# An attention layer's gathers: end rows picked by turned one-hots on TensorE, a small table for the other ends, and mixing by group with an operand in PSUM

## The chip, the cores and the metric

The kernel runs on one core of one Trainium2 chip. The metric is device time in microseconds for one execution; three runs of the kernel before gave 4565.82, 4569.41 and 4575.6 us, median 4569.41. The profile is of one further execution.

## The reference

12500 nodes with 256 features, 200000 edges (src, dst) sorted by dst. Two residual blocks follow each other: a graph convolution network and an attention layer. Cut to what matters:

```python
# block 0: y = two graph convolutions (sum over edges and self loop, scaled by degree) between two dense layers
h = relu(layernorm(x))
x = x + gcn(h)                       # out[d] = sum over edges (s, d) of norm * (h @ W)[s], twice
# block 1: attention
h = relu(layernorm(x))
xt = (h @ weight).reshape(-1, 4, 64)             # 4 heads of 64
alpha_l = einsum('ehd,hd->eh', xt[src], attn_l)
alpha_r = einsum('ehd,hd->eh', xt[dst], attn_r)
alpha = softmax(leaky_relu(alpha_l + alpha_r, 0.01), axis=1)
tmp = einsum('nh,nhd->nd', alpha[:n], xt[dst[:n]])   # edge i of the first n = 12500 edges goes to node i
x = x + broadcast(tmp to the 4 heads)
```

So the attention uses the first 12500 edges only. Since the edges are sorted by dst, their dst ends are a few low node numbers, whereas their src ends lie anywhere.

## The kernel before, in words

Nodes are cut into NT = 98 tiles of P = 128, edges into NCH = 112 chunks of CE = 1792 = J x P edges, J = 14. The program is written in the order in which each engine executes it; the tile framework adds the semaphores, but doesn't reorder.

*Preparation* (lines 484 to 757) loads the edges, brings them to the layout "edge on partition" (src_t, dst_all; base_b is the first dst of each chunk, repeated on all partitions), counts degrees, and norms x into table1 in HBM. Lines 753 to 755 make the index tiles dst_i and al_i of the attention.

*Two convolutions* (`convolve`, line 776) run over all 1563 edge tiles. For each, POOL issues an indirect DMA that gathers 128 rows of the table (`fgot`, L871, 64 buffers ahead), and PE multiplies them by a one-hot matrix of the chunk (`fhot`, made by DVE at L815) into an accumulator (L876). After a chunk `close` copies the sums out, turns them (L828) and adds them into a sliding buffer (L838). When the buffer's first 128 nodes are complete, `shift` opens the next window (L850, L851) and puts the steps of `finish` on a list `due`; each step has a due time counted in edge tiles, and `run` emits what is due after each tile. After the last tile `run()` emits the rest in the order of due times: this is the drain. If two windows are complete at once, the second is shifted J = 14 tiles later (line 860).

`finish2` (line 921), for the second convolution, has the steps a to r: SP loads the self rows, a root row and x rows (L933, L935, L939), then come two dense layers (fpz L952, fpo L964), x2 is stored in `kept_x` (SP, L971), normed, turned and multiplied by the attention weights with attn_l and attn_r folded in (fpx, L997, 264 columns: 256 of xt, 4 left, 4 right), copied (L1002) and written by ACT's queue to table3 (L1003). The PSUM tiles fpt, fpz, fpo and fpx have one buffer each.

*Attention* (lines 1012 to 1059) runs over NG = 14 groups of G = 7 node tiles. For each tile POOL gathers the 264 columns of the dst row (L1021) and the 4 left columns of the src row, from table3 seen as rows of 4 (L1024). SP loads the group's x rows (L1028, three buffers). DVE adds the two terms, takes the leaky maximum and the softmax over the 4 heads (L1031 to L1041, the exponential on ACT), and then per tile multiplies, sums over the heads and adds to x (L1046, L1049, L1050). SP stores the group (L1056, the incomplete last tile by L1059). POOL and DVE run ahead by the buffers: 2 for the gathered rows, 3 for the left columns.

Of the kernel before, what the change touches and what calls it, by code (L numbers as in the profile page):

```python
# [17 lines left out]
P = 128  # L18
# [395 lines left out]
def fast_path(  # L414
# [41 lines left out]
    DA = D + 2 * H  # L456
    G = 7
# [12 lines left out]
    table3 = dram.tile([NT * P, DA], F32, name="ftable3")  # L470
# [15 lines left out]
    dst_i = const.tile([P, NT], I32, name="fdst_i")  # L486
    al_i = const.tile([P, NT], I32, name="fal_i")
# [10 lines left out]
    with tc.tile_pool(name="fprep", bufs=1) as prep, \  # L498
# [102 lines left out]
        base_b = prep.tile([P, NCH], F32, name="base_b")  # L601
# [65 lines left out]
        with tc.tile_pool(name="fln", bufs=2) as ln:  # L667
            for g in range(NG):
# [71 lines left out]
                for i in range(G):  # L740
# [12 lines left out]
        nc.vector.tensor_copy(dst_i, dst_all[:, :NCH, :].rearrange("p c j -> p (c j)")[:, :NT])  # L753
        nc.vector.tensor_scalar(al_i, src_t.rearrange("p c j -> p (c j)")[:, :NT],
                                float(DA // H), float(D // H), op0=ALU.mult, op1=ALU.add)
# [10 lines left out]
    with tc.tile_pool(name="fwork", bufs=2) as work:  # L766
        for i, a in enumerate((attn_l, attn_r)):
# [8 lines left out]
    def convolve(ep, table, stride, width, ahead, with_sum, psum, finish):  # L776
# [42 lines left out]
        def close(c, acc, t):  # L819
# [24 lines left out]
            def shift(now):  # L844
# [14 lines left out]
                if state["w"] < complete[c + 1]:  # L859
                    at(now + J, shift)  # L860
# [66 lines left out]
    def finish2(psum, w, buf, sbuf):  # L927
# [65 lines left out]

        def q():
            px = v["px"] = psum.tile([P, DA], F32, name="fpx", bufs=1)
            for k in range(KC):
                nc.tensor.matmul(px, v["ht"][:, k, :], wg[:, k, :],  # L997
                                 start=(k == 0), stop=(k == KC - 1))

        def r():  # L1000
            xa = work.tile([P, DA], F32, name="fxa")
            nc.scalar.activation(xa, v["px"], AF.Copy)  # L1002
            nc.scalar.dma_start(table3[w * P:(w + 1) * P, :], xa)  # L1003
# [3 lines left out]

    with tc.tile_pool(name="psum2", bufs=1, space=PSUM) as psum, \
            tc.tile_pool(name="edges2", bufs=1) as ep, \
            tc.tile_pool(name="fwork2", bufs=2) as work:  # L1010
        convolve(ep, table2, D, D, 64, False, psum, lambda w, b, s: finish2(psum, w, b, s))


    left = table3[:].rearrange("n (a h) -> (n a) h", h=H)
    with tc.tile_pool(name="fatt", bufs=2) as ap:
        for t0 in range(0, NT, G):
            g = min(G, NT - t0)
            xa = ap.tile([P, G, DA], F32, name="fxg", bufs=2)
            al = ap.tile([P, G, H], F32, name="fal", bufs=3)
            for j in range(g):  # L1020
                nc.gpsimd.indirect_dma_start(  # L1021
                    out=xa[:, j, :], out_offset=None, in_=table3[:],
                    in_offset=bass.IndirectOffsetOnAxis(ap=dst_i[:, t0 + j:t0 + j + 1], axis=0))
                nc.gpsimd.indirect_dma_start(  # L1024
                    out=al[:, j, :], out_offset=None, in_=left,
                    in_offset=bass.IndirectOffsetOnAxis(ap=al_i[:, t0 + j:t0 + j + 1], axis=0))
            xr = ap.tile([P, G, D], F32, name="fxr", bufs=3)
            nc.sync.dma_start(xr[:, :g, :], kept_x[t0 * P:(t0 + g) * P, :].rearrange(  # L1028
                "(c p) d -> p c d", p=P))
            s = ap.tile([P, G, H], F32, name="fs")  # L1030
            nc.vector.tensor_add(s[:, :g, :], al[:, :g, :], xa[:, :g, D + H:])  # L1031
            nc.vector.scalar_tensor_tensor(s[:, :g, :], s[:, :g, :], SLOPE, s[:, :g, :],
                                           op0=ALU.mult, op1=ALU.max)
            m = ap.tile([P, G], F32, name="fm")
            nc.vector.tensor_reduce(m[:, :g], s[:, :g, :], AX.X, ALU.max)
            nc.vector.tensor_sub(s[:, :g, :], s[:, :g, :],
                                 m[:, :g, None].to_broadcast([P, g, H]))
            nc.scalar.activation(s[:, :g, :], s[:, :g, :], AF.Exp)
            nc.vector.tensor_reduce(m[:, :g], s[:, :g, :], AX.X, ALU.add)
            nc.vector.reciprocal(m[:, :g], m[:, :g])  # L1040
            nc.vector.tensor_mul(s[:, :g, :], s[:, :g, :],  # L1041
                                 m[:, :g, None].to_broadcast([P, g, H]))
            res = ap.tile([P, G, D], F32, name="fres", bufs=2)
            for j in range(g):
                part = ap.tile([P, H, C], F32, name="fpart")
                nc.vector.tensor_mul(part, xa[:, j, :D].rearrange("p (h c) -> p h c", h=H),  # L1046
                                     s[:, j, :, None].to_broadcast([P, H, C]))
                mix = ap.tile([P, C], F32, name="fmix")
                nc.vector.tensor_reduce(mix, part.rearrange("p h c -> p c h"), AX.X, ALU.add)  # L1049
                nc.vector.tensor_add(res[:, j, :].rearrange("p (h c) -> p h c", h=H),  # L1050
                                     xr[:, j, :].rearrange("p (h c) -> p h c", h=H),
                                     mix[:, None, :].to_broadcast([P, H, C]))
            n0, n1 = t0 * P, min((t0 + g) * P, N)
# [4 lines left out]
            if r:  # L1058
                nc.sync.dma_start(out[n0 + k * P:n1, :], res[:r, k, :])  # L1059

# [40 lines left out]
```

## Time and profile before

| | us |
|---|---|
| median of the runs shown | 4569.41 |
| the profiled execution | 4561.96 |
| its span, first to last instruction | 4559.9 |
| PE busy | 3245.4 (71%) |
| POOL busy | 3182.4 (70%) |
| DVE busy | 1201.9 (26%) |
| ACT busy | 368.2 (8%) |
| first gather of the first convolution at | 288.86 |
| first gather of the second convolution at | 2270.95 |
| first gather of the attention at | 4282.26 |

An instruction group in the profile shows its line, engine, operation and tiles, its count, its busy time and the mean duration. The time of a gather on POOL is that of its issue, not of its transfer. Gathers: L871 3126 times at 954 ns, L1021 98 times at 987 ns, L1024 98 times at 996 ns. PE: L876 6252 times at 482 ns (each fp32 matmul is two instructions). DVE in the attention: L1046 419 ns, L1049 584 ns, L1050 426 ns, 98 each; L815 makes a chunk's one-hot in 2000 ns. The windows view gives the busy time of each engine in a stretch, the critical chain what each instruction on the path that ended last was released by, and the timeline every instruction in order.

### The profile page before, as it was taken

Reading aid. Unit: us, or ns where it says so; the run is one execution under the profiler, and the core shown is the slowest. Engines: PE = TensorE matmul, PEld = TensorE weight load, DVE = VectorE, ACT = ScalarE, POOL = GpSimd, SP = SyncE. Lnnn points to the kernel's source line nnn. Section 1 sums busy time; section 2 is a strip of 40 time slices with the busy share of each in tenths; the row PEclk is TensorE's granted clock in tenths of the full one; section 3 lists DMA queues with packets and bytes.
Section 4 is the critical chain, followed back from the end, with each engine's and each line's share of the span. In section 5 each row is a group of like instructions: output and inputs, shape, how many; then the busy total and the mean of one; then the engine's idle time right before and its main releaser. Section 6 shows DMA issues by size and latency. Waiting matters only on the chain.

```text
span 4559.9 us, 37494 instructions
## 1 busy us (share of the span) xinstructions
PE 3245.4 (71%) x12108; PEld 1986.7 (44%) x12108; DVE 1201.9 (26%) x2736; ACT 368.2 (8%) x956; POOL 3182.4 (70%) x3334
## 2 busy tenths in 40 slices
PE   4557777777777777777777888888878788778400
PEld 3533334434444443443345555555545555555200
DVE  4322222222222222222212222222222222222255
ACT  1210000000000000000001111111111111111100
POOL 0037777777777777777677777777777777777476
PEclk7558888888888888788879888888898998998655
DMA  2344444444444444444334444444444444444354
GB/s 76 115 119 119 119 119 120 120 120 119 119 119 122 118 120 118 120 121 118 108 116 132 130 130 131 130 134 129 130 133 129 132 129 134 128 132 129 92 152 144
DMA packets 302161, 561.52 MB, mean 123 GB/s; under 512 B 71717, under 2 KB 198564, under 8 KB 301956
## 3 DMA queue, kind: packets, MB, share of 16 engines
q0 software_dynamic: 157888, 426.59, 33.6%
q1 hardware_dynamic: 113918, 104.77, 7.5%
q10 hardware_dynamic: 30150, 27.68, 1.8%
q8 instruction: 98, 1.61, 0.1%
q14 instruction: 107, 0.88, 0.1%
HBM read 493.89 MB, written 64.78 MB: 123 GB/s over the span
## 4 chain that ended last, share of the span: by engine, by line
DMA 43%; PE 33%; issue 11%; POOL 7%; DVE 4%; ACT 1%; SPq 0%; POOLq 0%; ACTq 0%; DVEq 0%
DMA fgot<-ftable,fsrc_t 38%; PE facc L876 20%; POOL fgot L871 6%; PE fpz L952 2%; DMA fxt<-in_x_dram 2%; PE fpo L911 2%; PE fpz L954 2%; PE fpo L964 2%; PE fpx L997 1%; DMA fxr<-kept_x 1%; PE fpt L886 1%; PE fpo L912 1%; ACT h L741 1%; PE fpo L965 1%; DVE fmix L1049 1%
## 5 line engine op out<-in xcount | busy, mean ns | idle before, releaser
L871 POOL DMA_INDIRECT fgot<-ftable,fsrc_t x3126 | 2982.8, 954 | 1251.2 <-issue 717.2
L876 PE MATMUL facc<-fgot,fhot 128*128 128x257 f32 (+1 forms) x6252 | 2310.9, 482 | 874.7 <-DMA fgot<-ftable,fsrc_t 858.2
L876 PEld LDWEIGHTS facc<-fgot,fhot 128*128 128x128 f32 x6252 | 1167.3, 221 | 1853.3 <-DMA fgot<-ftable,fsrc_t 1675.4
L815 DVE TENSOR_TENSOR fhot<-iota_p,to_t 128x1792 f32<-128x1792 f32 x224 | 447.6, 2000 | 0.1
L969 DVE SCALAR_TENSOR_TENSOR fx<-fpo,fdinv,fxb 128x256 f32<-128x256 f32 x98 | 47.4, 484 | 1206.2 <-PE fpo L965 1206.2
L822 ACT ACTIVATE fsums<-facc 128x257 f32<-128x257 f32 (+1 forms) x224 | 86.2, 385 | 2914.1 <-PE facc L876 2914.1
L905 DVE TENSOR_TENSOR fin<-buf,fpt 128x256 f32<-128x256 f32 x98 | 41.3, 421 | 1010.8 <-PE fpt L901 1010.8
L838 DVE TENSOR_TENSOR buf<-buf,fturn 128x256 f32 x224 | 94.5, 422 | 641.2 <-PE fturn L830 530.9
L952 PE MATMUL fpz<-fin,fwb 128*128 128x128 f32 x784 | 157.9, 334 | 0.0
L1021 POOL DMA_INDIRECT fxg<-ftable,fdst_i x98 | 96.8, 987 | 72.0 <-PEq L1071 42.4
L911 PE MATMUL fpo<-wf,fin 128*128 128x256 f32 x392 | 139.4, 493 | 1.8 <-DVE fin L905 1.8
L952 PEld LDWEIGHTS fpz<-fin,fwb 128*128 128x128 f32 x784 | 130.9, 235 | 16.2 <-issue 5.7
L699 PE MATMUL count<-hot_a,hot_b 128*16 128x20 bf16 (+2 forms) x1591 | 62.2, 206 | 105.3 <-DVE hot_a L688 105.3
L997 PE MATMUL fpx<-fwg,ht 128*128 128x264 f32 x392 | 119.7, 434 | 0.5 <-ACT ht L992 0.5
L1024 POOL DMA_INDIRECT fal<-ftable,fal_i x98 | 97.6, 996 | 29.9 <-issue 29.2
L911 PEld LDWEIGHTS fpo<-wf,fin 128*128 128x128 f32 x392 | 102.4, 262 | 25.2 <-ACT fo L916 2.6
L964 PE MATMUL fpo<-fwo,fz 128*128 128x256 f32 x392 | 110.7, 409 | 0.0
L954 PE MATMUL fpz<-rm,fb2r 1*128 1x128 f32 x392 | 110.1, 366 | 0.0
L699 PEld LDWEIGHTS <-hot_b 128*16 128x16 bf16 x1591 | 61.7, 106 | 105.6 <-DVE hot_b L688 91.8
L997 PEld LDWEIGHTS fpx<-fwg,ht 128*128 128x128 f32 x392 | 85.4, 219 | 17.0 <-ACT ht L992 0.7
L828 PE MATMUL fturn<-fident,fsums 128*128 128x128 f32 x448 | 91.5, 288 | 0.0
L964 PEld LDWEIGHTS fpo<-fwo,fz 128*128 128x128 f32 x392 | 83.6, 213 | 15.6
(147 smaller groups left out, 1757.9 us busy)
## 6 DMA issues: line engine op xcount, KB each, us to landing
fgot<-ftable,fsrc_t POOLq DMA_INDIRECT x3126, 2.8
ftable<-fxa ACTq DMA_DIRECT2D x98, 132.0 KB
ftable<-h SPq DMA_DIRECT2D x14, 910.0 KB
self<-ftable SPq DMA_DIRECT2D x98, 130.0 KB
ftable<-fo ACTq DMA_DIRECT2D x98, 128.0 KB
self<-ftable SPq DMA_DIRECT2D x98, 128.0 KB
kept_x<-fx SPq DMA_DIRECT2D x98, 128.0 KB
fxr<-kept_x SPq DMA_DIRECT2D x14, 896.0 KB
```

The source lines that it names most:

```text
L699: nc.tensor.matmul(count[i][:, o:o + m], hot_b[:, :, t], hot_a[:, at:at + m, t], start=False, stop=False, skip_group_check=True)
L815: nc.vector.tensor_tensor(h[:, :n, :], iota_p[:, None, :].to_broadcast([P, n, P]), to_t[:, c, :n, None].to_broadcast([P, n, P]), ALU.is_equal)
L838: nc.vector.tensor_add(b, b, v["pt"][:, :KC, :])
L871: nc.gpsimd.indirect_dma_start(out=got, out_offset=None, in_=table[:], in_offset=bass.IndirectOffsetOnAxis(ap=src_t[:, c, j:j + 1], axis=0))
L876: nc.tensor.matmul(acc, hots[c][:, j, :], got[:, :width], start=(j == 0), stop=(j == nj[c] - 1))
L911: nc.tensor.matmul(po, v["f"][:, k, :], wf[:, k, :], start=(k == 0), stop=False)
L952: nc.tensor.matmul(pz[:, m, :], wb[:, k, m * P:(m + 1) * P], v["f"][:, k, :], start=(k == 0), stop=False)
L954: nc.tensor.matmul(pz[:, m, :], b2r[:, m * P:(m + 1) * P], v["rm"], start=False, stop=True)
L964: nc.tensor.matmul(po, v["z"][:, m, :], wo[:, m, :], start=(m == 0), stop=False)
L997: nc.tensor.matmul(px, v["ht"][:, k, :], wg[:, k, :], start=(k == 0), stop=(k == KC - 1))
L1021: nc.gpsimd.indirect_dma_start(out=xa[:, j, :], out_offset=None, in_=table3[:], in_offset=bass.IndirectOffsetOnAxis(ap=dst_i[:, t0 + j:t0 ...
L1024: nc.gpsimd.indirect_dma_start(out=al[:, j, :], out_offset=None, in_=left, in_offset=bass.IndirectOffsetOnAxis(ap=al_i[:, t0 + j:t0 + j + ...
```

## The change

Only what the attention reads is changed, and how it is made.

Two tables take the place of table3. `table_l` has the 4 left columns of all nodes. `table_r` has xt and the 4 right columns (260 columns) of the first XW = 9 windows only, which hold all dst ends of the AC = 7 chunks that the attention uses. Windows from the ninth on compute just 4 columns of fpx. For this the order of the folded columns is turned, right before left.

For each of the 7 chunks one indirect DMA gathers 128 rows of table_r, from the chunk's first dst onwards (`rows`). `turn_hots` loads the chunk's 1792 dst into every partition and compares them with base + partition: a one-hot with the row on the partition and the edge along the free side. `ends_of` then multiplies it, tile by tile, by the chunk's rows on PE and copies the result on ACT; it runs two groups ahead of `mix`. Three one-hots are made ahead of the second convolution, the other four when `ends_of` first needs them. POOL gathers only the left columns, directly by src.

`mix` does product, sum over heads and addition once per group of 7 tiles (1792 elements) instead of once per tile. The shares of the heads and the mixed sums lie in PSUM.

In both convolutions a second window that is complete at the end is shifted 3 tiles after the first instead of 14.

```diff
+    DR = D + H
-    table3 = dram.tile([NT * P, DA], F32, name="ftable3")
+    AC = -(-N // CE)
+    XW = (M * (AC - 1) + OFF + P - 1) // P + 1
+    table_r = dram.tile([XW * P, DR], F32, name="table_r")
+    table_l = dram.tile([NT * P, H], F32, name="table_l")
...
-        nc.vector.tensor_copy(dst_i, dst_all[:, :NCH, :].rearrange("p c j -> p (c j)")[:, :NT])
-        nc.vector.tensor_scalar(al_i, src_t.rearrange("p c j -> p (c j)")[:, :NT],
-                                float(DA // H), float(D // H), op0=ALU.mult, op1=ALU.add)
+        nc.vector.tensor_scalar(row_i, base_b[:, :AC], lane, float(XW * P - 1), op0=ALU.add,
+                                op1=ALU.min)
...
-                    at(now + J, shift)
+                    at(now + (J if c + 1 < NCH else 3), shift)
...
+        d0 = 0 if w < XW else DR
         def q():
             px = v["px"] = psum.tile([P, DA], F32, name="fpx", bufs=1)
             for k in range(KC):
-                nc.tensor.matmul(px, v["ht"][:, k, :], wg[:, k, :],
+                nc.tensor.matmul(px[:, d0:], v["ht"][:, k, :], wg[:, k, d0:],
                                  start=(k == 0), stop=(k == KC - 1))
         def r():
             xa = work.tile([P, DA], F32, name="fxa")
-            nc.scalar.activation(xa, v["px"], AF.Copy)
-            nc.scalar.dma_start(table3[w * P:(w + 1) * P, :], xa)
+            nc.scalar.activation(xa[:, d0:], v["px"][:, d0:], AF.Copy)
+            nc.scalar.dma_start(table_l[w * P:(w + 1) * P, :], xa[:, DR:])
+            if w < XW:
+                nc.scalar.dma_start(table_r[w * P:(w + 1) * P, :], xa[:, :DR])
...
+    def turn_hots(c):
+        to_all = ap.tile([P, CE], I32, name="to_all", bufs=2)
+        nc.sync.dma_start(to_all, dst[c * CE:(c + 1) * CE].partition_broadcast(P))
+        hot_t[c] = ap.tile([P, CE], F32, name="hot_t", bufs=3)
+        nc.vector.tensor_scalar(hot_t[c], to_all, base_b[:, c:c + 1], lane,
+                                op0=ALU.subtract, op1=ALU.is_equal)
...
+        for c in range(3):
+            turn_hots(c)
         convolve(ep, table2, D, D, 64, False, psum, lambda w, b, s: finish2(psum, w, b, s))
...
+        for c in range(AC):
+            rows.append(mp.tile([P, DR], F32, name="rows", bufs=AC))
+            nc.gpsimd.indirect_dma_start(
+                out=rows[c], out_offset=None, in_=table_r[:],
+                in_offset=bass.IndirectOffsetOnAxis(ap=row_i[:, c:c + 1], axis=0))
+        def ends_of(g):
+            xa = ends[g] = mp.tile([P, G, DR], F32, name="fxg", bufs=4)
+            for i in range(G):
+                c, j = divmod(g * G + i, J)
+                if j == 0 and c not in hot_t:
+                    turn_hots(c)
+                px = psum.tile([P, DR], F32, name="fends", bufs=4)
+                nc.tensor.matmul(px, hot_t[c][:, j * P:(j + 1) * P], rows[c], start=True,
+                                 stop=True)
+                nc.scalar.activation(xa[:, i, :], px, AF.Copy)
+        def mix(g):
+            xa, t0 = ends.pop(g), g * G
+            al = mp.tile([P, G, H], F32, name="fal", bufs=3)
+            for i in range(G):
+                c, j = divmod(t0 + i, J)
+                nc.gpsimd.indirect_dma_start(
+                    out=al[:, i, :], out_offset=None, in_=table_l[:],
+                    in_offset=bass.IndirectOffsetOnAxis(ap=src_t[:, c, j:j + 1], axis=0))
+            xr = mp.tile([P, G, D], F32, name="fxr", bufs=3)
+            nc.sync.dma_start(xr, kept_x[t0 * P:(t0 + G) * P, :].rearrange(
+                "(c p) d -> p c d", p=P))
...
+            share = psum.tile([P, G, H], F32, name="share")
+            nc.vector.tensor_mul(share, s, m[:, :, None].to_broadcast([P, G, H]))
+            part = mp.tile([P, G, H, C], F32, name="fpart")
+            nc.vector.tensor_mul(part, xa[:, :, :D].rearrange("p g (h c) -> p g h c", h=H),
+                                 share[:, :, :, None].to_broadcast([P, G, H, C]))
+            mixed = psum.tile([P, G, C], F32, name="fmix")
+            nc.vector.tensor_reduce(mixed, part.rearrange("p g h c -> p g c h"), AX.X, ALU.add)
+            res = mp.tile([P, G, D], F32, name="fres", bufs=2)
+            nc.vector.tensor_add(res.rearrange("p g (h c) -> p g h c", h=H),
+                                 xr.rearrange("p g (h c) -> p g h c", h=H),
+                                 mixed[:, :, None, :].to_broadcast([P, G, H, C]))
...
+        for g in range(NG + 2):
+            if g < NG:
+                ends_of(g)
+            if g >= 2:
+                mix(g - 2)
```

## The prediction

> **What bounds the kernel now.** I read the page's chain of waits first, then the busy time by windows, then the timeline around the last gather and the attention stage. The chain says which work the two convolutions hang on:
>
> ```profile
> DMA fgot<-ftable,fsrc_t 38%; PE facc L876 20%; POOL fgot L871 6%; PE fpz L952 2%; DMA fxt<-in_x_dram 2%; PE fpo L911 2%; PE fpz L954 2%; PE fpo L964 2%; PE fpx L997 1%; DMA fxr<-kept_x 1%; PE fpt L886 1%; PE fpo L912 1%; ACT h L741 1%; PE fpo L965 1%; DVE fmix L1049 1%
> ```
>
> The gathers and the matmuls waiting for them carry it. That it is the gathers' pace and not the matmuls' shows in the windows: POOL is busy equally in both convolutions, though PE has more to do in the second.
>
> ```profile
> 1000.00:1500.00 500.00, 374.28 (x1108) 205.17 (x1108) 110.01 (x236) 19.87 (x53) 378.78 (x399) 0.85 0.43 120
> 3000.00:3500.00 500.00, 409.21 (x1494) 268.67 (x1494) 125.17 (x255) 56.76 (x153) 379.05 (x398) 0.88 0.45 131
> 4300.00:4400.00 100.00, 0.00 (x0) 0.00 (x0) 57.21 (x151) 1.36 (x6) 76.44 (x78) 0.50 0.50 145
> ```
>
> After the window come PE, PEld, DVE, ACT and POOL with counts, clock, DMA share and GB/s. 398 gathers in 500 us are one per 1.25 us, so 1563 gathers make 1960 us per convolution. PE work removed there buys nothing.
>
> The third row is the attention stage: no PE, POOL at its full pace. It holds 14 groups of 7 node tiles, two gathers a tile. From the timeline it runs from 4282.26 (first gather) to 4559.9: 277.6 us, with 42 us of drain between the last edge gather at about 4240 and it. In the critical chain of one of its periods the reader should see that POOL is not alone:
>
> ```profile
> 4372.70 8.46 DMA fxr<-kept_x
> 4381.18 0.05 DVEq L1050
> ...
> 4389.76 0.44 DVE fres L1050
> 4390.22 0.38 SPq L1056
> 4390.59 0.05 issue
> 4390.64 8.47 DMA fxr<-kept_x
> ```
>
> SP works in order: the load of the next group's x rows (L1028) stands behind the store of this group's result (L1056), which waits for the last addition. The load takes 8.47 us, and only then can the 21 mixing operations (8.9 us) run on, since the first addition waits for it. 0.45 + 8.47 + 0.13 + 8.9 = 17.95 us; the 14 gathers need 14 x 1.25 = 17.5, more where they take 1.41. Two bounds nearly tie at 18 us per group, so a change has to lower both.
>
> **What the skill says.** SBUF, section "Who interferes with whom": a DVE instruction with two SBUF inputs contends with a GpSimd instruction that reads SBUF, one with a single SBUF input does not. The trace fits: an attention gather takes 0.94 us beside an idle DVE and 1.11 beside the mixing, whose multiplications and additions read two SBUF tiles. VectorE: DVE Perf Modes, "The perf-mode tier table": fp32 tensor_tensor and tensor_reduce run at one element a cycle, an SBUF tensor_scalar at two; here 1568 elements took 1.73 us in a tensor_tensor (L632) and 0.97 in a tensor_scalar (L607). DMA: Bandwidth & Descriptors, "Issuing engines are not separate DMA queues": all issuers share 16 engines. In the load's window they are 0.89 busy and 0.22 outside it:
>
> ```profile
> 4390.60:4399.10 8.50, 0.00 (x0) 0.00 (x0) 2.33 (x9) 0.23 (x1) 6.37 (x8) 0.50 0.89 264
> 4399.10:4408.20 9.10, 0.00 (x0) 0.00 (x0) 8.49 (x19) 0.00 (x0) 6.97 (x8) 0.50 0.22 61
> 4537.10:4544.20 7.10, 0.00 (x0) 0.00 (x0) 2.33 (x9) 0.23 (x1) 0.00 (x0) 0.50 0.85 260
> ```
>
> The third row is the last load, without gathers: load and store of 0.9 MB each keep 16 engines 0.85 x 7.1 = 6.0 us, 3.0 us each.
>
> **The change, part by part.**
>
> (1) Gathers of the attention: 196 become 7 (row ends) + 98 (L-table). The 7 need a table finished early and run in the drain, where POOL idles. The 98 keep the price of the present small gathers: 7 x 1.25 = 8.75 us a group.
>
> (2) Row ends on PE and ACT: 98 fp32 products of 260 columns and 98 copies. A pair of such matmuls took 0.43 us back to back and 0.9 at the half clock (L876); a copy of 264 took 0.39. A group is 3 to 6.3 us PE and 2.7 us ACT, below every other bound. The first three groups come ahead of the first mixing: 4 x 0.9 + 17 x 0.45 = 11 us from the end of PE's drain, which the first gathers cover.
>
> (3) Mixing by group on DVE: seven small operations and the exponential as now, 1.8 us (4301.06 to 4302.87). The product over 1792 elements with one PSUM operand: 2.0, the price of L815, which has the same size and a PSUM operand. The addition: 2.0 likewise. The reduction to 448 outputs in PSUM is not shown; L538 reduces 1792 to one in 2.0, and L1049 is 0.17 us over a plain 256-element operation for 64 outputs, or 2.6 ns an output, which makes 3.1. Bounds 2.2 (extra paid once) and 3.3; I take 3.1. Sum with gaps 9.05 us, instead of 1.8 + 7 x 1.41 = 11.7. What matters more: of this only the 2.0 us of addition now comes after the load.
>
> (4) An ordinary period is then 0.45 + load + 0.13 + 2.0. The load: 7.06 without gathers, 8.47 with 14 of them; the first stage's loads of the same size, beside a store and no gathers, took 6.9 to 8.8. I take 7.7: 10.3 us, above POOL's 8.75 and DVE's 9.05. So SP's order becomes the sole bound.
>
> (5) The turned one-hots. Each needs a load of 1792 indices into all 128 partitions (0.9 MB, on SP's queue) and one tensor_scalar of 1792: 0.97 x 1792/1568 = 1.1 us at two elements a cycle, 2.0 at one; I take 1.5. Three are made ahead of the second convolution, but chunks 3 to 6 are made inside the attention, at groups 6, 8, 10, 12. There the broadcast load stands on SP behind the store of the mixing before, and its DVE operation stands ahead of the next mixing: small operations, product and reduction, which otherwise hide under the x load, wait for it. The broadcast lands after the store and itself have been moved: 1 + 3 + 3 and some gathers, 7.3 us. (Bounds: 6.0 if 7 KB rows move faster; 16 if it goes at the rate of the only broadcast in the trace, 0.13 MB in 3.8 us with perhaps 2 fixed, times 7.) Such a period is 0.45 + 7.3 + 1.5 + 9.05 = 18.3 us, four times; the x load hides in it.
>
> (6) The sum of the stage, from the first small gather: seven gathers and landing 10.1 (now 4282.26 to 4301.06 for fourteen is 18.8, less 7 x 1.25), first mixing 9.05, nine periods of 10.3 = 92.7, four of 18.3 = 73.2, and the tail 8.0 (6.7 now from the last DVE end, but then most of the store had left). 193.0 us against 277.6.
>
> (7) Drain of the second convolution. Its last window is shifted 3 steps after the one before instead of 14, so its chain of loads, matmuls and norms interleaves with the previous window's; windows from the ninth on write 4 columns of fpx, not 264 (the last took 2.14 us in the chain, then about 0.5). Walking the 26 us of PE steps in the new order, with each single-buffer PSUM wait, the last write leaves 4 us earlier (1 to 7). The first convolution has the same edit but no long chain: 0.5 (-1 to 1.5). Inside the convolutions the smaller fpx and table writes are hidden under the gathers.
>
> (8) Three turned one-hots before the second convolution: 2.7 MB on SP and 3 DVE operations meet the last table2 write, for which the first gather waits. I charge 2 us (0 to 6). PE starts some us late but has 20% slack and 64 buffers of gathers.
>
> (9) Fewer instructions in the preparation (dst_i, al_i): below 1 us.
>
> Sum: 277.6 - 193.0 + 4 + 0.5 - 2 = 87 us. The profiled execution took 4561.96 us, 2.06 outside its span of 4559.9; it becomes 4475. The median of the runs is 4569.41, 7.45 above the profiled one, so the forecast against it is 4482.
>
> **Rivals.**
> (a) SP's order costs nothing: loads and broadcasts are early enough, and DVE with 9.05 us per group is the bound. 13 x 9.05 + 4 x 1.5 = 124 instead of 166: 4440. For it: x and index buffers are free early. Against: the program order on SP is plain, and DVE waited for the x load in 9 of 14 groups, 43.5 us. Chance 0.08.
> (b) The broadcasts are slow, 16 us each, all readers at the same 7 KB: four periods of 27: 35 us more, 4517. For it the small broadcast's 3.8 us. Chance 0.12.
> (c) Slower than before: the same reads crowd one spot of memory so much that a broadcast takes 40 us. Four of them on SP, with DVE behind: 4 x 32.7 = 131 more, 4613. It decides from 7.3 + 87/4 = 29 us on. For it only that no row shows a broadcast of this size; against it, 0.13 MB in 3.8 us. Chance 0.05.
> (d) PE stays at half clock and the ends are the bound, 7 x 0.9 plus copies through four buffers: at 9 us still hidden; at 12 it would give 4500, inside the range.
>
> **How the numbers follow.** Forecast 4482 with 0.73; the rivals as above, and 0.02 for no change by losses that nobody foresaw. Faster is 0.73 + 0.08 + 0.12. Good ends together (load 7.06, broadcast 6.0, reduction 2.2, one-hot 1.1, drain and start) give 22 us less, the bad (8.47, 10, 3.3, 2.0) 28 more: 4460 to 4510. Part of (a) and most of (b) widen it to 4448 to 4518. Faster by over 0.2% (9 us, about what this measurement can tell from none) 0.93, within 0.02, slower 0.05.
>
> **What would show it.** Right: x load still the longest piece of the attention's chain, ordinary periods near 10, four near 18 with DVE waiting for the index broadcast; POOL pausing between groups; gathers never at 1.11 beside the mixing; the edge gathers still one per 1.25 us. Wrong: periods all alike, a broadcast over 10 us, a reduction of 2 us, the first gather of the second convolution over 5 us late.

## The result, and the profile after

| | before | after |
|---|---|---|
| median of 4 runs, us | 4570.33 | 4502.25 |
| ratio, 95% interval | | 0.9854 [0.9837, 0.9871] |
| profiled execution, us | 4561.96 | 4503.18 |
| its span, us | 4559.9 | 4501.2 |

68 us less in the median, where the forecast had 87. The chain of waits of the changed kernel, by line:

```profile
DMA fgot<-ftable,fsrc_t 19%; PE facc L883 10%; POOL fgot L878 3%; PE fpz L959 2%; PE fpz L961 2%; PE fpo L971 1%; PE fpt L893 1%; PE fpo L972 1%; PE fpx L1007 1%; POOL fal L1068 1%; PE fends L1059 1%; DMA fxr<-kept_x 0%; DVE fmix L1090 0%; PE fturn L835 0%; DVE fpart L1087 0%
```

This line must not be laid beside that of before share by share. By engine its shares sum to 50 percent, because the chain is followed back only through the second convolution (it begins at 2249 us). Within that half nothing is new. The windows tell the halves apart (PE, PEld, DVE, ACT, POOL busy with counts, clock, DMA share, GB/s):

```profile
1000.00:1500.00 500.00, 373.51 (x1107) 202.72 (x1106) 108.57 (x230) 19.86 (x53) 379.12 (x397) 0.85 0.44 119
3000.00:3500.00 500.00, 384.83 (x1496) 249.11 (x1494) 125.65 (x255) 51.11 (x153) 378.74 (x399) 0.91 0.48 125
4300.00:4400.00 100.00, 29.40 (x91) 22.36 (x90) 65.58 (x81) 19.20 (x58) 61.88 (x66) 0.63 0.49 139
```

The convolutions stand at 397 and 399 gathers in 500 us, as before, although PE is busy 24 us less in the second row. In the attention POOL has come down from 76 to 62 of 100 us and DVE is up to 66: no engine is full, so the stage hangs on waits.

From the starts of SP's stores in the timeline, the periods between one group's store and the next are 10.05, 10.58, 9.78, **22.72**, 9.83, **23.39**, 10.22, **23.71**, 10.46, **23.74**, 9.83, 9.62, 10.17 us. Before they lay at 15 to 21. The four long ones are where a new one-hot is made, and their length is the surprise. The timeline of the first of them (start, duration, engine, line, and in brackets the idle time ahead and its releaser):

```profile
4339.80 0.38 SPq L1098 DMA_DIRECT2D out_dram<-fres  x1
...
4340.23 0.56 SPq L1025 DMA_DIRECT2D to_all<-in_dst_dram  x1
4340.89 1.08 SPq L1072 DMA_DIRECT2D fxr<-kept_x  x1
...
4347.40 1.21 DVE L1027 TENSOR_SCALAR hot_t<-to_all,base_b,lane 128x1792 f32<-128x1792 int32 x1 [7.62 <-DMA to_all<-in_dst_dram]
...
4348.71 8.29 PE L1059 MATMUL fends<-rows,hot_t 128*128 128x260 f32 x28 [24.93 <-issue]
...
4349.19 0.19 DVE L1079 TENSOR_TENSOR fs<-fs,fm 128x28 f32<-128x28 f32 x1
4349.96 0.39 ACT L1061 ACTIVATE fxg<-fends 128x260 f32<-128x260 f32 x1 [18.89 <-PE fends L1059]
...
4353.10 1.26 ACT L1061 ACTIVATE fxg<-fends 128x260 f32<-128x260 f32 x3 [0.15 <-PE fends L1059]
...
4354.26 0.22 ACT L1080 ACTIVATE fs<-fs 128x28 f32<-128x28 f32 x1
...
4354.51 0.18 DVE L1081 TENSOR_REDUCE fm<-fs 128x7 f32<-128x28 f32 x1 [5.13 <-ACT fs L1080]
...
4355.19 2.02 DVE L1087 TENSOR_TENSOR fpart<-fxg,share 128x1792 f32<-128x1792 f32 x1
...
4357.24 3.19 DVE L1090 TENSOR_REDUCE fmix<-fpart 128x448 f32<-128x1792 f32 x1
...
4360.47 2.02 DVE L1092 TENSOR_TENSOR fres<-fxr,fmix 128x1792 f32<-128x1792 f32 x1
...
4362.52 0.38 SPq L1098 DMA_DIRECT2D out_dram<-fres  x1
```

The broadcast and the compare are as forecast: 7.6 us of waiting, 1.2 of compare. Then DVE prepares the softmax and stops again for 5.1 us (6.0 to 6.2 in the other three), for the exponential on ACT. Its input was ready at 4349.4, but ACT works in order too. `ends_of` is called ahead of `mix`, so seven copies of row ends (L1061) stand ahead of the exponential, and they wait for PE, whose matmuls could start only when the new one-hot was there, and at first at half clock: 0.54 was granted in their first 4.2 us, with the copies 0.87 us apart, and 1.00 after. The row ends for a group two later hold back the mixing of this one.

The second surprise is at the start of the attention, in POOL's timeline:

```profile
4234.49 0.94 POOL L878 DMA_INDIRECT fgot<-ftable,fsrc_t  x1 [0.30 <-issue]
4281.14 0.94 POOL L1045 DMA_INDIRECT rows<-table_r,row_i  x1 [45.71 <-DMA table_l<-fxa]
...
4288.63 0.95 POOL L1045 DMA_INDIRECT rows<-table_r,row_i  x1 [0.30 <-issue]
4289.88 0.94 POOL L1068 DMA_INDIRECT fal<-table_l,fsrc_t  x1 [0.30 <-issue]
```

The seven row gathers don't run in the drain. They wait through it for the last write of table_l, which they don't read, and then hold up the small gathers for 8.7 us.

Stage by stage the span went down as follows.

| stage | after less before, us |
|---|---|
| to the first gather of the first convolution | -0.8 |
| from there to the first of the second | +3.3 |
| the 1563 gathers of the second | -6.9 |
| from its last gather to the first gather of the attention | +3.3 |
| row gathers | +8.7 |
| first small gather to the end (277.6 to 211.3) | -66.3 |
| sum | -58.7 |

The medians differ by 68 and not 59, since the profiled execution of before lay 8.4 us under its median and that of after 0.9 above.

### The profile page after: what moved, and what is told of

It reads as the page before. It is cut to its first block, busy times and chain, and to the rows that moved or that the text cites. A ratio compares the mean times of both kernels' runs of the same rounds, so it can differ in the third digit from the quotient of the medians.

```text
span 4501.2 us, 37677 instructions
## 1 busy us (share of the span) xinstructions
PE 3232.3 (72%) x12304; PEld 1967.8 (44%) x12304; DVE 1178.5 (26%) x2490; ACT 384.8 (9%) x1054; POOL 3082.6 (68%) x3244
## 4 chain that ended last, share of the span: by engine, by line
DMA 20%; PE 19%; issue 6%; POOL 4%; DVE 1%; ACT 0%; POOLq 0%; DVEq 0%; ACTq 0%; SPq 0%
DMA fgot<-ftable,fsrc_t 19%; PE facc L883 10%; POOL fgot L878 3%; PE fpz L959 2%; PE fpz L961 2%; PE fpo L971 1%; PE fpt L893 1%; PE fpo L972 1%; PE fpx L1007 1%; POOL fal L1068 1%; PE fends L1059 1%; DMA fxr<-kept_x 0%; DVE fmix L1090 0%; PE fturn L835 0%; DVE fpart L1087 0%
## 5 line engine op out<-in xcount | busy, mean ns | idle before, releaser
L878 POOL DMA_INDIRECT fgot<-ftable,fsrc_t x3126 | 2977.7, 953 | 1251.8 <-issue 690.0
L883 PEld LDWEIGHTS facc<-fgot,fhot 128*128 128x128 f32 x6252 | 1154.2, 220 | 1939.3 <-DMA fgot<-ftable,fsrc_t 1762.8
L1059 PE MATMUL fends<-rows,hot_t 128*128 128x260 f32 x196 | 61.3, 485 | 118.3 <-issue 98.4
L1068 POOL DMA_INDIRECT fal<-table_l,fsrc_t x98 | 93.0, 949 | 75.1 <-DVE fs L1076 47.1
L959 PE MATMUL fpz<-fin,fwb 128*128 128x128 f32 x784 | 137.8, 301 | 0.5 <-ACT fz L966 0.5
L971 PE MATMUL fpo<-fwo,fz 128*128 128x256 f32 x392 | 120.6, 435 | 0.7 <-DVE fx L976 0.7
L959 PEld LDWEIGHTS fpz<-fin,fwb 128*128 128x128 f32 x784 | 111.9, 204 | 15.3 <-issue 2.4
L1059 PEld LDWEIGHTS fends<-rows,hot_t 128*128 128x128 f32 x196 | 48.0, 250 | 131.3 <-issue 108.4
L961 PE MATMUL fpz<-rm,fb2r 1*128 1x128 f32 x392 | 99.3, 334 | 0.0
L893 PE MATMUL fpt<-fident,self 128*128 128x128 f32 x392 | 94.2, 328 | 1.4 <-PE fpt L908 0.9
L858 DVE COPY buf<-buf 128x640 f32<-128x640 f32 x196 | 86.5, 442 | 0.0
```

The lines of the kernel that those rows point to most:

```text
L878: nc.gpsimd.indirect_dma_start(out=got, out_offset=None, in_=table[:], in_offset=bass.IndirectOffsetOnAxis(ap=src_t[:, c, j:j + 1], axis=0))
L883: nc.tensor.matmul(acc, hots[c][:, j, :], got[:, :width], start=(j == 0), stop=(j == nj[c] - 1))
L893: nc.tensor.transpose(pt[:, k, :], s[:, k * P:(k + 1) * P], ident)
L959: nc.tensor.matmul(pz[:, m, :], wb[:, k, m * P:(m + 1) * P], v["f"][:, k, :], start=(k == 0), stop=False)
L961: nc.tensor.matmul(pz[:, m, :], b2r[:, m * P:(m + 1) * P], v["rm"], start=False, stop=True)
L971: nc.tensor.matmul(po, v["z"][:, m, :], wo[:, m, :], start=(m == 0), stop=False)
```

## The experiments

Two theories to begin with. One: the missing time is in the four long periods (ACT's order behind the new one-hot) and in the row gathers, which wait because their tile lies in memory that the convolution's pools had and whose last reader is the write of table_l. Its rival: each of these waits covers another, so that removing it gives little. All ratios are to the kernel before, run on the same chip.

The first four kernels ran on a chip on which TensorE's granted clock is 0.71 on average, gathers come one per 1.43 us, and the kernel before itself takes 5198 us. The changed kernel was not run there, so only stages and the four kernels among themselves can be read.

**Row gathers in memory of their own**

```diff
-            rows.append(mp.tile([P, DR], F32, name="rows", bufs=AC))
+            rows.append(ap.tile([P, DR], F32, name="rows", bufs=AC))
```

`ap` is the pool that was open during the convolution.

> The seven gathered row tiles move to the memory pool that is open since before the second convolution; nothing else changes. In the changed kernel these gathers stood idle for 45.7 us until the last write of table_l and then took 8.74 us ahead of the first gather of left columns. Theory A (they wait for memory that the second convolution's tiles give up only at its end): they now run right after the last edge gather, the first left-column gather comes about 1 us after the last table_l write, and the time falls by about 8.5 us, to 4494. Theory B (they wait because the two tables are written by the same queue): they still wait until the last table_l write and the time stays within 2 us of 4502.

5138.74 us, 0.9887 [0.9871, 0.9904]. The row gathers start at 4804.35, one cadence after the last edge gather (4803.09); the first small gather comes 2.3 us after the last table write (4894.77). The wait was that of reused memory. What it costs in time is measured beside the changed kernel, below.

**One-hots turned one group earlier**

```diff
             if g < NG:
                 ends_of(g)
+            c = (g + 1) * G // J
+            if c < AC and c not in hot_t:
+                turn_hots(c)
```

(The new lines go behind `ends_of(g)` in the last loop, ahead of `mix`.)

> The four one-hots that fall inside the attention are made one group earlier, after that group's matmuls and copies are in the queues; loads, compares and their number stay. Theory A (the four long periods of about 23 us have two parts: DVE waits 7.5 us for the broadcast, and the exponential stands on ACT behind seven copies that wait for matmuls that wait for the new one-hot, about 5 us): the second part goes, the long periods become 18 us, and the time falls by 4 x 5 = 20 us, to 4482. Theory B (the exponential is late for another reason, the left columns or PE's cold clock): the long periods stay near 23 us and the time near 4502.

5120.38 us, 0.9854 [0.9834, 0.9873]. The long periods are 17.79, 17.82, 17.87 and 18.02, the others 9.6 to 11.0. The other three kernels on this chip have long ones of 22.4 to 23.8, 23.2 on average (and two of them a slow first period besides, 29.3 and 18.3). Its timeline shows the same broadcast and the same compare, but the exponential with nothing ahead of it:

```profile
4976.61 1.21 DVE L1027 TENSOR_SCALAR hot_t<-to_all,base_b,lane 128x1792 f32<-128x1792 int32 x1 [7.40 <-DMA to_all<-in_dst_dram]
...
4978.67 0.23 ACT L1080 ACTIVATE fs<-fs 128x28 f32<-128x28 f32 x1 [14.67 <-DVE fs L1079]
4978.93 0.18 DVE L1081 TENSOR_REDUCE fm<-fs 128x7 f32<-128x28 f32 x1 [0.35 <-ACT fs L1080]
...
4979.16 0.39 ACT L1061 ACTIVATE fxg<-fends 128x260 f32<-128x260 f32 x1 [0.26 <-issue]
```

The copies now come after it, and DVE waits 0.35 us instead of 5. So some 5.4 us of each long period is ACT's order, and what is left is the 18 us of the forecast. The time agrees: it is 22 and 25 us under those of the two kernels that follow, which keep the long periods and the late row gathers, and 4 x 5.4 are 22.

**The late shift at 14 tiles, and fpx at full width**

```diff
-                    at(now + (J if c + 1 < NCH else 3), shift)
+                    at(now + J, shift)
```

> The last window of both convolutions is shifted 14 tiles after the one before again, as in the kernel before; the rest is as changed. Theory A (the prediction: interleaving the last two windows shortens the drain by about 4 us): the time rises by about 4 us, to 4506. Theory B (the interleaved order packs nothing, since single-buffered PSUM tiles and PE's order make the two windows wait for each other, and the small fpx leaves PE at its low clock): the drain, now 44.5 us from the last edge gather's issue to the last table write, stays or becomes up to 4 us shorter, and the time 4498 to 4502.

5142.38 us, 0.9897 [0.9879, 0.9914].

```diff
-        d0 = 0 if w < XW else DR
+        d0 = 0
```

The second kernel computes and copies columns that nobody reads.

> All windows compute and copy the full 264 columns of fpx again, though only 4 are stored from the ninth on; the rest is as changed. The second convolution's gathers took 1961.0 us in the changed kernel and 1967.9 before, the drain after them 3 us more than before. Theory A (both are PE's doing: less work lets PE keep up better, but idles it into the lower clock in the drain): the gathers take 1967 again, the drain 3 us less, and the time rises by about 4 us, to 4506. Theory B (the 7 us are chance collisions of gathers with other work, and the drain is set by the new order of steps): the gathers' time moves without pattern by a few us, the drain becomes 1 to 2 us longer for the larger product, and the time is 4500 to 4508.

5145.84 us, 0.9901 [0.9886, 0.9917]. Both intervals overlap that of the row gathers' kernel, and the drains, 87 and 91 us on this chip against 87 and 92 in the other two, don't order by the edit. The second convolution's gathers took 2240 us in all four kernels, so the full fpx didn't bring the 7 us back that it was to explain. Neither part can be weighed here; the shift was tried again below.

The next four kernels ran on a chip on which before took 4568.35.

**All one-hots inside the second convolution**

```diff
+            if w % 4 == 1 and w // 4 < AC:
+                load_ends(w // 4)
...
+            if w % 4 == 1 and w // 4 < AC:
+                turn_hots(w // 4)
...
-        for c in range(3):
-            turn_hots(c)
-        convolve(ep, table2, D, D, 64, False, psum, lambda w, b, s: finish2(psum, w, b, s))
+        convolve(ep, table2, D, D, 56, False, psum, lambda w, b, s: finish2(psum, w, b, s))
```

`load_ends` is the broadcast, in step a of `finish2`, and `turn_hots` the compare, in step i; hot_t has seven buffers, and eight buffers of gathers make room for them.

> All seven one-hots are made within the second convolution: a broadcast load in window 1, 5, ... 25 and its compare 28 tiles later, seven buffers instead of three; for their memory the convolution's gathers run 56 tiles ahead instead of 64 and one index buffer is left. Theory A (the four long periods come from the one-hots alone): all thirteen periods of the attention become about 10 us, which takes 4 x 12.9 = 51 us, and the start of the second convolution 1 to 2 us more; the time falls to 4450. Theory B (SP's order or PE with the copies bound these groups anyway): periods of 12 to 18 us stay where a new one-hot is first used, and the time stays above 4475. If 56 buffers are too few, POOL's gathers are slower than one per 1.256 us.

4457.86 us, 0.9761 [0.9744, 0.9777]. All periods are 9.7 to 11.2. The stage from the first small gather takes 157.9 us instead of 211.3, that is 53.4 less, or 13.4 for each long period. The second convolution takes 1965.3, 4.3 more than in the changed kernel. Whole: about 42 us less than the changed kernel (0.9854 - 0.9761, times 4568; the two ratios are from two chips).

**Mixing by group alone, on the kernel before**

```diff
-            for j in range(g):
-                part = ap.tile([P, H, C], F32, name="fpart")
...
+            share = psum.tile([P, G, H], F32, name="share")
+            nc.vector.tensor_mul(share, s, m[:, :, None].to_broadcast([P, G, H]))
...
+            mixed = psum.tile([P, G, C], F32, name="fmix")
+            nc.vector.tensor_reduce(mixed, part.rearrange("p g h c -> p g c h"), AX.X, ALU.add)
```

> The kernel before with one part of the change: the mixing over a group at once with shares and mixed sums in PSUM. All 196 gathers, table3 and the drain stay as before. Theory A (POOL's 14 gathers a group, 17.5 us, are the second of two nearly equal bounds): a group still takes 17.5 to 17.9 us, the gathers lose their 1.11 us forms, and the time falls by 3 to 8 us, to 4562 to 4567. Theory B (the mixing was the bound): a group takes 10 to 12 us and the time falls by 80 us.

4556.68 us, 0.9976 [0.9969, 0.9983]. A group takes 17.1 to 18.7 us and no gather of the attention over 0.96, as in Theory A. The time falls by 11.7 us, more than the 3 to 8 of that theory.

**The change without mixing by group**: all the rest of it, with the seven-fold loop of before in `mix`.

> The changed kernel with the mixing per tile again, as before: three operations of 256 elements for each of the seven tiles, no PSUM operand. Tables, ends on PE and the drain stay changed. Theory A (SP's order and the mixing are the other bound): an ordinary period is 0.45 + 7.2 + 0.13 + 8.9 = 16.7 us, and less only by what the small gathers no longer take; the four long ones reach 0.45 + 7.2 + 1.2 + 0.85 + 5.1 + 0.9 + 9.9 = 25.6. The time rises by 9 x 6.6 + 4 x 2.8 = 70 us, to about 4572, the same as the kernel before. Theory B (the gathers saved were the gain): it stays below 4530.

4567.41 us, 0.9999 [0.9990, 1.0008]. Ordinary periods are 15.7 to 17.3, long ones 25.2 to 26.2.

The two halves of the change are worth 11.7 us and nothing; together they brought 68 on the first chip and 60 on the last. In the first half, POOL runs at its pace through the whole period, and DVE has its three operations done early and waits for a gather:

```profile
4426.03 2.02 DVE L1050 TENSOR_TENSOR fres<-fxr,fmix 128x1792 f32<-128x1792 f32 x1
...
4436.71 0.19 DVE L1032 TENSOR_TENSOR fs<-fal,fxg 128x28 f32<-128x28 f32 x1 [8.66 <-DMA fxg<-ftable,fdst_i]
```

In the second half POOL has time, but DVE waits for the x load with 19 of its 21 operations still to do:

```profile
4350.76 0.43 DVE L1093 TENSOR_TENSOR fres<-fxr,fmix 128x256 f32<-128x256 f32 x1 [5.66 <-DMA fxr<-kept_x]
```

In this kernel the row gathers started 45 us before the last table write went out (4284.55). They waited too, but for 6.5 us and for something else, DVE's copy of the convolution's sliding buffer:

```profile
4239.85 0.94 POOL L1045 DMA_INDIRECT rows<-table_r,row_i  x1 [6.47 <-DVE buf L858]
```

They don't read that buffer either. The one edit makes `fpart` and `fmix` smaller, so the row tiles probably lie elsewhere (the addresses are not on record). This speaks for reused memory once more: which foreign operation a gather waits for changed with the size of a third tile.

**The x load ahead of the store**

```diff
-            xr = mp.tile([P, G, D], F32, name="fxr", bufs=3)
-            nc.sync.dma_start(xr, kept_x[t0 * P:(t0 + G) * P, :].rearrange(
-                "(c p) d -> p c d", p=P))
+            if g + 1 < NG:
+                load_x(g + 1)
+            xr = xrs.pop(g)
```

(`load_x` is the load that stood here, as a function; that of group 0 goes ahead of the loop.)

> The changed kernel with one change of SP's order: the x rows of the next group are requested ahead of the store of this group. Theory A (SP's order sets the ordinary periods, DVE's 9.05 us come next): the nine ordinary periods go from 10.0 to about 9.1, the waits of the addition for x vanish, the long periods stay, as the broadcast's place behind the store stays, and the time falls by 8 to 10 us, to 4493. Theory B (the transfers themselves are the limit): loads take longer by what they start earlier, periods stay at 10 and the time at 4502.

4495.53 us, 0.9846 [0.9830, 0.9863]. The nine ordinary periods are 9.1 to 9.2: DVE's own 9.05 and gaps. The nine sum to 81.9 us instead of 90.5. In the changed kernel the addition waited for x in each of them, 9.0 us in all; here it never does. The first line is of the changed kernel, the second of this one:

```profile
4327.97 2.02 DVE L1092 TENSOR_TENSOR fres<-fxr,fmix 128x1792 f32<-128x1792 f32 x1 [1.50 <-DMA fxr<-kept_x]
```

```profile
4325.73 2.02 DVE L1102 TENSOR_TENSOR fres<-fxr,fmix 128x1792 f32<-128x1792 f32 x1
```

It was SP's order that made them ten. The whole time shows it less clearly: the changed kernel had ratios of 0.9854 and 0.9863 on two other chips, so this edit alone is worth 4 to 8 us, and the intervals overlap.

The last four kernels ran on one chip, the changed one among them; before took 4564.14.

**The changed kernel, again**

> The changed kernel itself, on the chip of the other three. Expected: ratio to the kernel before 0.985, drain 44 us, four long periods of 23.4, nine ordinary of 10.1. If the drain differs from 44.5 by more than 3 us in this profile, drain lengths of single profiles cannot be compared, and only times can.

4504.37 us, 0.9863 [0.9844, 0.9882]; the long periods are 22.0 to 23.6, the others 9.8 to 10.5. But its drain, from the last edge gather to the last table write, took 48.4 us in this profile and 44.5 in the first: the same code differs by 4 us. The clock granted in it was 0.56 here and 0.64 there.

**Row gathers in memory of their own, again**

> Row gathers into memory of their own, once more, to be read beside the changed kernel on the same chip. Theory A (their wait for the last table write is that of reused memory, and their 8.7 us lie on the path): row gathers issued within 2 us of the last edge gather, the first small gather 2 to 4 us after the last table write instead of about 11, and the time 8 to 9 us below the changed kernel. Theory B (the seven gathers only fill time in which the last table write lands): time within 3 us of the changed kernel.

4495.95 us, 0.9845 [0.9828, 0.9861]: 8.4 less than the changed kernel beside it. The first small gather comes 2.35 us after the last table write instead of 10.9.

```profile
4239.19 0.95 POOL L878 DMA_INDIRECT fgot<-ftable,fsrc_t  x1 [0.30 <-issue]
4240.44 0.95 POOL L1045 DMA_INDIRECT rows<-table_r,row_i  x1 [0.30 <-issue]
...
4287.37 0.94 POOL L1068 DMA_INDIRECT fal<-table_l,fsrc_t  x1 [38.45 <-PE fends L1059]
```

The last line names PE as releaser. This gather uses nothing that those products make, and it reads the table whose last write had gone out 2.35 us earlier; where a wait is for several semaphores, the profile names the one that came last. The same gather of the kernel with mixing by tile has the table's write as its releaser.

**The shift at 14 tiles, again**

> The second window at the end is shifted 14 tiles after the first again, as before the change, to be read beside the changed kernel on the same chip. Theory A (the earlier shift interleaves two windows and shortens the drain): drain from last edge gather to last table write 4 us longer than in the changed kernel, time 4 us longer. Theory B (it makes the drain's matmuls queue up behind each other): drain and time shorter by 3 to 4 us. Theory C (it does nothing, the differences of the drain are the matmul clock's): within 2 us.

4505.16 us, 0.9865 [0.9848, 0.9881]: medians 0.8 us apart, as in Theory C, lowest runs 6.0 apart, which is no more than single runs scatter. The drain took 50.3 us at a granted clock of 0.53:

```profile
4239.12:4289.41 50.29, 40.44 (x124) 27.53 (x122) 11.14 (x38) 8.95 (x25) 0.95 (x1) 0.53 0.14 34
```

With the early shift it took 48.4 us at 0.56 (above) and 52.1 at 0.50 (the kernel with mixing by tile), so this drain lies between them in length as in clock. No gain from the earlier shift is shown.

**All three repairs together**: one-hots in the convolution (48 buffers of gathers), rows in their own memory, x load ahead of the store.

> Three edits on top of the changed kernel: all one-hots made inside the second convolution, the row gathers in memory of their own, and the x load of the next group ahead of the store. Theory A (three separate costs on one path: one-hots about 45, row gathers about 8.7, and the wait for the x load about 1 us in each of thirteen periods): the gains add, all thirteen periods become 9.1 us, the row gathers are issued within 2 us of the last edge gather, the ratio to the kernel before is about 0.971, that is 4435 on a chip where that takes 4568. Theory B (the gains share one cover, for example the transfers of loads and stores meet or 48 buffers of gathers are too few): periods stay at 10 or above or the second convolution gets over 5 us longer, and the ratio is 0.975 or above.

4433.95 us, 0.9716 [0.9695, 0.9736]: 70.4 less than the changed kernel beside it. In the profiles the stage from the first small gather takes 147.0 us instead of 209.4, and the wait between the last table write and that gather 3.1 instead of 10.9: 70.1 less together, while the spans differ by 68.2. Twelve of thirteen periods are 9.09 to 9.21, one is 10.38. DVE hardly stops:

```profile
4304.92:4387.00 82.08, 48.32 (x126) 35.90 (x126) 75.41 (x90) 22.36 (x72) 61.96 (x67) 0.75 0.70 203
```

75.4 of 82.1 us busy (the columns are those of the windows above). These were separate costs on one path: from the last table write to the end, the one-hots, the x load and the row gathers alone took 53.1, 9.6 and 7.6 us off the changed kernel's profile, 70.3 in sum. So the three small edits gain 70 us on top of the 60 that the change brings on this chip. The second convolution, now with seven broadcasts and 48 buffers of gathers, takes 1964.4 us, 5.1 more than in the changed kernel beside it.

## Why the prediction was right, and where its sum was off

The mechanism and the sign held: the end came from the attention, two bounds were lowered together, and SP's order became the bound of the ordinary period. The forecast was 20 us too low; term by term against the two profiled executions, the planned 87 became 58.7.

**(1) Row gathers that "run in the drain, where POOL idles": failed, +8.7.** The step asked whether the table is finished early and whether POOL idles, and both were so. It didn't ask where the destination lies. The row tiles came from a pool opened after the convolution, and waited 45.7 us for the last table write, whose source must have had their memory. In a pool that was open before they didn't wait, on two chips.

**(5) The long period, 18.3 forecast, 23.4 measured: +20.4 over four.** The broadcast (7.3 forecast, 7.4 to 7.6 waited) and the mixing were right, and the compare took 1.21 where 1.5 was taken. The failure is in step (2), which has the work of PE and ACT "below every other bound". It is, by its load: ACT has 2.7 us of copies to do in a period. But the copies sit in order on ACT ahead of an instruction on the path, and they wait for the very one-hot that is late. With the order changed, the period is 17.8 to 18.0, where 0.45 + 7.4 + 1.2 + 9.05 gives 18.1.

**(3), (4) The ordinary period: right.** 10.3 forecast, nine sum to 90.5 instead of 92.7. The mixing's product and addition took 2.02 each (2.0), and the reduction, which no row had shown, 3.20 (3.1, bounds 2.2 to 3.3). The Trainium skill, VectorE: DVE Perf Modes, "The perf-mode tier table", has tensor_reduce at the same single tier as tensor_tensor; here 1792 elements took 3.20 us in the strided reduction and 2.02 in the product, so the tier alone doesn't price it. The estimate of 2.6 ns for each output was the better guide; whether the outputs or the strided input cost it, no run separates. After the load only the addition remained, as said. (The 8.9 us that the text has for 21 operations behind the load before are those of 19: the first product and reduction ran ahead of it, and all 21 take 7 x 1.41 = 9.9.)

**(6) First mixing and tail: right**, 19.5 and 7.8 us where 19.15 and 8.0 stood.

**(7) Drain "4 us earlier": not seen, +7.3 in these two profiles.** From the last edge gather to the first of the attention the time grew by 3.3. But the windows of the drain show another thing that changed. They are, in turn, of before, of the changed kernel, and of mixing by group alone, whose drain is the code of before:

```profile
4238.90:4279.48 40.58, 30.05 (x125) 20.54 (x124) 11.15 (x38) 9.91 (x25) 0.94 (x1) 0.88 0.26 81
```

```profile
4234.49:4278.98 44.49, 36.60 (x130) 25.39 (x129) 11.41 (x38) 9.00 (x26) 0.94 (x1) 0.64 0.14 38
```

```profile
4237.78:4288.58 50.80, 42.38 (x126) 28.40 (x124) 11.15 (x38) 10.02 (x25) 0.94 (x1) 0.63 0.20 65
```

The granted clock was 0.88 in the first and 0.64 in the second, and PE is busy 6.6 us longer in the second with less work. The third has the clock of the second, and there the code of before takes 50.8 us: at like clock the changed drain is the shorter one by 6 us, nearly all of it PE's busy time. The time without PE is 10.5, 7.9 and 8.4. So much of the drain is matmul time at whatever clock is granted, and one profile against another can't show 4 us there. The step may have been right but for the clock, and then by the narrower products rather than by the shift, which showed nothing; that is not shown. The Trainium skill, TensorE: Matmul & The Clock Gate, "Part 1: The HAM clock gate", has the array at half rate until it has been busy for some microseconds. The trace agrees in size: one instruction of L1059 took 382 ns at its fastest and 802 at its slowest, and in the long period shown above the clock rose from 0.54 to 1.00 after 4.2 us of work. Why before's profiled drain kept the clock was not tried. That execution lay 8.4 us under its median, so most runs of before may well have had a longer drain.

**(8), (9) and the first convolution: nearly right.** The second convolution's first gather came 2.5 us later, where the terms left some 1.5 (2 for the one-hots, less 0.5 for the first convolution; the preparation's share was not put in the sum): +1.0.

**Not in the sum at all: -6.9.** The 1563 gathers of the second convolution took 1968.0 before and 1961.0 after. The kernels with the narrow table writes and the first three one-hots ahead lie at 1959.3 to 1962.0 on two other chips with the faster clock, those with the wide writes (before, and mixing by group alone) at 1966 and 1968. The step called the smaller writes "hidden under the gathers"; the gathers seem to have run freer beside them. No run separates the writes from the narrower matmuls; fpx at full width was to do it, but ran only on the chip where all kernels took 2240.

87.1 - 8.7 - 18.3 (stage, the 20.4 among it) - 7.3 - 1.0 + 6.9 = 58.7. So against the profiled time the forecast was 28 us low (4475 against 4503.18). The 7.45 us that the text added for the way from the profile to the median are not there in the changed kernel, whose profiled execution lies at its median; they hid eight of the 28, and the 6.9 that nobody had planned kept the 28 from being 35. That the forecast is off by only 20 is in part luck.

**The rivals.** (a), SP's order costing nothing, is what the x load ahead of the store makes true, not what the change does. (b) and (c), slow broadcasts: the wait was 7.6 us at most. (d) named PE at half clock as a bound by its load; the half clock did lengthen the wait of ACT, by the order and not by the load.

Of the signs that the text named, most came: ordinary periods near 10, DVE waiting for the index broadcast, POOL pausing between groups, edge gathers one per 1.25 us. Two failed: the long periods are not near 18, and the x load is not the longest piece of the attention's chain. From 4278 us to the end it has 9.7 percent, the small gathers 11.0 and the matmuls of the row ends 10.7.

The gathers' 1.11 us beside the mixing are gone, as the text said: 0.94 to 0.96 in the changed kernel's ordinary periods, and about 1.1 again for a fifth of them with the mixing by tile. That is what the Trainium skill, SBUF — State Buffer, "Who interferes with whom", has on operations with two SBUF inputs. What the text did not foresee is that the compare of a one-hot, which reads one SBUF tile, slows a gather more: 1.43 us at 4347.30 in the changed kernel, and 1.24 to 1.75 in each of the seven profiles that have a gather issued beside a compare. Why it does, no run shows.

## What to carry to other kernels

Work that is hidden by its load must be checked for its place: an instruction that waits on an in-order engine delays all behind it, so look for the one on the path that was issued after it. A load that is to run early needs memory that is free early, and not only data that is ready; put it into a pool that was open then. Where two bounds tie, halves of a change tried alone show little: here 12 and 0 us, together 60 to 68.

## What was not expected of the hardware

- One chip granted TensorE 0.71 of its clock through the whole kernel, and 0.72 and 0.75 in windows of the convolutions where 0.85 and 0.91 stood in the changed kernel's first profile. Gathers came 350 in 500 us instead of 398, and the kernel before took 5198 us against 4570. That the matmuls then set the pace is what the chain suggests, and was not tried.
- Where nothing held it up, an indirect gather of 128 rows cost POOL one cadence of 1.25 us whatever it moved: rows of 1 KB (L878), 1040 bytes (L1045) and 16 bytes (L1068) all took 0.94 to 0.95 us of issue and 0.30 between.
- A load of one 7 KB row of indices into all 128 partitions, 0.9 MB, was there 7.2 us after its issue with a store of 0.9 MB ahead of it, no slower than a plain load of that size (6.98 to 7.53 for x).
